# A two-layer graph kernel: another order for the last four tiles of step 0, and a tail with more of its small work on VectorE

## The chip, the cores and the metric

The kernel runs on one core of one Trainium2 chip. The metric is device time in microseconds (us), lower is better: the median of 3 runs before the change is 1654.93 us (1652.97 to 1655.37). Five engines work from queues of their own, each in order: PE (TensorE, matrix products), DVE (VectorE), ACT (ScalarE), POOL (GpSimd, which also issues the gathers and scatters by index) and SP (which issues plain transfers).

## The reference

There are 3327 rows of 256 numbers. Layer 0 is graph attention over a sparse adjacency with a gated update and a layer norm. Layer 1 does two steps of the following, and ends in a layer norm:

```python
def _top_p_attention(X, W1, W2, W3):
    q = X @ W1.T @ W2.T
    k = X @ W3.T
    probs = softmax(q @ k.T)                       # (3327, 3327)
    sp, idx = probs sorted downwards, and its order
    cs = jnp.cumsum(sp, axis=-1)
    keep_sorted = cs - sp < 0.9                    # the nucleus of each row
    A = probs * (mask of what is kept)
    return A / jnp.maximum(A.sum(-1, keepdims=True), 1e-12)

R = (adj + I) / row sums;  Z = 0;  Xf = Xa = X
for n in range(2):
    A = _top_p_attention(Xa, W1, W2, W3)
    Xf = R @ Xf
    Xa = A @ Xa
    Z = Z + Xf @ U1[n].T + Xa @ U2[n].T
out = layernorm(X + Z)
```

## The kernel before, in words

The rows are cut into 26 tiles of 128 (the last has 127). The code orders every engine's queue by the order in which instructions are recorded (`manual_schedule`), so the order of the text, made by generators that yield to each other, is the order on each engine.

**Step 0** (`sparse`, `parts_0`, `step_0`). The attention of this step is so peaked that a tile of rows needs at most 640 columns. A tile goes through some 50 named parts: logits (`logits`, `copy`, on PE and ACT), the nucleus limit (`settle_1`, `settle_2` on DVE), which columns anybody needs (`sign`, `count`, `places`, `hot_l/h/b` on DVE, `placed` on PE, `node` on ACT), the list written to memory and read back in another layout (`told` on DVE, then two SP transfers; `index` on POOL), five gathers (`needed0..4`, POOL, L1598), then `turned` (PE transposes L1623), `turned_copy` (ACT L1630), `by_nodes` (PE L1637), `weights` (ACT L1645), `kept` (DVE L1650), `attention` (PE L1656), `one_over` (DVE), `xa` (ACT L1669), `qk0..3` (PE and ACT: q and k of step 1 for these rows), and `xa_u`, `c_out`, `c_add` (the product with U2: PE L1421, ACT L1690, POOL L1695). `ORDER_0` gives each part a tick; `sparse` starts a tile every 32 ticks (`EVERY0`), so part p of tile t comes at tick 32t + its own. `order_0(t)` makes exceptions for the last four tiles (NT is 26): `SOONER` puts their gathers at other ticks, `LATER` moves `c_add`, and for the last two tiles `KEPT_BACK` parts are left for after step 0. Beside the last tiles, `first_1` records the logits of step 1's first two tiles (`some_logits`: PE L1759, ACT L1762) and the eight largest of each group (`largest`: DVE L1775), each chunk of columns when enough tiles are done (`self.done`).

**Step 1** (`run`, the loop over `i`). Each of 26 tiles (i = 26 to 51) is one `product`: seven groups of transposes (`turn`, L2045, ACT copy L2047) and matmuls (`times`, L2061) with `xu`; between the groups, in seven `slots`, the other work is recorded: logits of tile i+3, the largest of i+2, and for i+1 the short list (`list_1`, `list_2`), the flag of rows that could not be settled by it (`told`, POOL L1820 to L1825), the masking of p (`mask`: DVE match_replace L1957, then a scalar_tensor_tensor with a sum, L1927), `put_aside_1` (POOL L2113 to L2130, with a small matmul `pos` on PE, L2116) and `put_aside_2` (DVE L2147 computes an index, POOL L2148 scatters the flagged rows' data into the table `left_over`). `one_over` (POOL L1936, L1937) is 1 over a row's sum. `tile_end` is the end of older tiles (layer norms by `by_sums` on ACT and POOL, store). `late` is the turn i = 50, in which the mask of the last tile is made; there the scatter stands between the match_replace and the sum.

**The flagged rows** ("hard" rows) are done again in two blocks of 128, h0 and h1, with longer lists: h0's rows are closed after tile 13, h1's after the last tile. `hard_load(k)` reads the table (SP L2158), makes the index (POOL L2161, L2162) and gathers the rows (POOL L2176). `hard_q`, `hard_exp` make their p. A bound on the threshold is sought in six cuts (`CUTS`): the first `COARSE[k]` of them by `coarse_bound` (four ACT passes over p, L2231, and seven or eight small instructions, L2237 to L2246), the rest by `bound` (one DVE pass over p, L1963, and three small ones). `hard(k)` then makes the list of 72, drops what is out (three match_replace passes, L1957) and sums what is kept (L2301); `hard_end(k)` is the product and the end of the rows; `hard_store` scatters them to the output. `COARSE` is (4, 1). `ends` is the last section: h0 is finished, then h1; `whole` makes one number from all flags (DVE L2523 to L2538, two small matmuls), by which a slow path is taken if any row stayed unsettled. The end of h1's rows is `output_rows`: `scaled`, then two layer norms in which ACT does the passes over the row (L2069, L2036), DVE the moments (L2005, L2007) and POOL the rest (L2070 to L2081).

Of the kernel before, what the change touches and what calls it, by code (L numbers as in the profile page):

```python
# [16 lines left out]
P = 128  # L17
# [76 lines left out]
SOONER = {"needed0": 123, "needed1": 124, "needed2": 125, "needed3": 126, "needed4": 127}  # L94
LATER = {"c_add": 196}


def order_0(t):

    order = [(SOONER.get(name, tick), name) if t >= NT - 2 else (tick, name) for tick, name in ORDER_0]  # L100
    if t >= NT - 2:
        order = [o for o in order if o[1] not in KEPT_BACK]
    elif t >= NT - 4:
        order = [(LATER.get(name, tick), name) for tick, name in order]
    return sorted(order, key=lambda o: o[0])
# [12 lines left out]
COARSE = (4, 1)  # L118
# [1120 lines left out]
class Layer1:  # L1239
# [477 lines left out]
    def first_1(self):  # L1717


        while self.phase <= EVERY0 * (NT - 1) + max(AT_0[k] for k in ("sign0", "sign1", "y_out")):  # L1720
            yield
        v = self.item(NT)
        self.item(NT + 1)
        self.fetch(NT)
        for pair in self.chunks():
            while self.done * P < min(NT * P, HALF + pair[0][1] + LC):
                yield
            for i in (NT, NT + 1):
                self.some_logits(i, pair)
                yield  # L1730
            for i in (NT, NT + 1):
                self.largest(i, pair)
                yield
        for b in range(EB):
            self.neighbour(NT, b)
# [63 lines left out]
    def settle(self, lst, before, last, thr2, r, drop, flag, tag, room=None):  # L1799
# [19 lines left out]
        engine = nc.vector if room_given else nc.gpsimd  # L1819
# [81 lines left out]
    def list_2(self, i):  # L1901
# [8 lines left out]
            v.lst, before[:r], v.last, v.thr2, r, DROP, self.flag[:r, n, v.at : v.at + 1], tag  # L1910
# [21 lines left out]
    def one_over(self, i):  # L1932
# [3 lines left out]
        nc.gpsimd.tensor_scalar(v.rA[:r], v.thr2[:r], 0.5e-12 / TOP_P, v.sA[:r], ALU.mult, ALU.max)  # L1936
        nc.gpsimd.tensor_tensor(v.rA[:r], v.rA[:r], self.minus_one[:r], ALU.pow)  # L1937
# [63 lines left out]
    def moments(self, src, r, tag):  # L2001

        nc = self.nc
        st = self.st.tile([P, nc.vector.BN_STATS_DIM], F32, tag="bn", name=f"bn{tag}")
        nc.vector.bn_stats(st[:r], src)  # L2005
        mv = self.st.tile([P, 2], F32, tag="mv" + tag[0], name=f"mv{tag}", bufs=4)
        nc.vector.bn_aggr(mv[:r], st[:r])  # L2007
        nc.gpsimd.tensor_scalar(mv[:r, 1:2], mv[:r, 1:2], 1.0, LN_EPS, ALU.mult, ALU.add)
        nc.gpsimd.tensor_tensor(mv[:r, 1:2], mv[:r, 1:2], self.power[:r], ALU.pow)
        return mv  # L2010

    def sums(self, h, r, tag):
# [7 lines left out]
        yield  # L2020
        sq = self.st.tile([P, 1], F32, tag="sq" + tag[0], name=f"sq{tag}", bufs=2)
# [7 lines left out]

    def shift(self, mv, r, tag):  # L2030
        shift = self.small("shift", f"shift{tag}")
        self.nc.gpsimd.tensor_scalar(shift[:r], mv[:r, 0:1], mv[:r, 1:2], -1.0, ALU.mult, ALU.mult)
        return shift[:r]

    def normalized(self, h, mv, shift, r):
        self.nc.scalar.activation(h, h, AF.Identity, bias=shift, scale=mv[:r, 1:2])  # L2036
# [35 lines left out]
    def output_rows(self, h, terms, r, tag):  # L2072

        nc = self.nc
        m = self.moments(h, r, f"a{tag}")
        shift = self.shift(m, r, f"a{tag}")
        yield
        self.normalized(h, m, shift, r)
        nc.gpsimd.tensor_tensor(h, h, self.g[:r], ALU.mult)
        for term in terms:  # L2080
            nc.gpsimd.tensor_tensor(h, h, term, ALU.add)  # L2081
        yield
        m = self.moments(h, r, f"b{tag}")
        shift = self.shift(m, r, f"b{tag}")
        yield
        self.normalized(h, m, shift, r)

# [20 lines left out]
    def put_aside_1(self, i):  # L2108
        nc, v = self.nc, self.items[i]
        t = v.at  # L2110
        flag = self.flag[:, 1, t : t + 1]
        flag16 = self.small("flag16", f"flag16_{t}", dtype=BF16)
        nc.gpsimd.tensor_copy(flag16, flag)  # L2113
# [6 lines left out]
        nc.gpsimd.tensor_scalar(v.far, flag, -1.0e6, self.base, ALU.mult, ALU.add)  # L2120
        flagged = self.small("flagged", f"flagged{t}")
        self.flagged16 = self.small("flagged16", f"flagged16_{t}", dtype=BF16)
        if self.flagged is not None:
            nc.gpsimd.tensor_tensor(flagged, self.flagged, flag, ALU.add)
        else:
            nc.gpsimd.tensor_copy(flagged, flag)
        nc.gpsimd.tensor_copy(self.flagged16, flagged)
        self.flagged = flagged
        nc.gpsimd.tensor_copy(v.pay[: v.r, 0:1], self.sh.rowid[: v.r, t : t + 1])
        nc.gpsimd.tensor_scalar(v.pay[: v.r, 3:4], v.lim[: v.r], v.t[: v.r], None, ALU.max)  # L2130
# [22 lines left out]
    def hard_load(self, k):  # L2153
# [7 lines left out]
        nc.gpsimd.tensor_copy(v.idx[:, 0:1], v.pay[:, 0:1])  # L2161
        nc.gpsimd.tensor_scalar(v.idx[:, 1:2], v.pay[:, 0:1], float(N - 1), None, ALU.min)  # L2162
# [19 lines left out]
    def hard_q(self, k):  # L2182

        nc, v = self.nc, self.items[f"h{k}"]
        xt = self.transposed((v.x[:, 0, :],), P, f"q{v.tag}")
# [15 lines left out]
        nc.gpsimd.tensor_scalar(v.top, v.pay[:, 3:4], 1.0001, None, ALU.mult)  # L2201
# [14 lines left out]
    def coarse_bound(self, k, cuts, junk):  # L2216


        nc, v = self.nc, self.items[f"h{k}"]
        less = self.small(f"less{k}", f"less{v.tag}")  # L2220
        nc.gpsimd.tensor_scalar(less, v.pay[:, 2:3], 0.5 * (1.0 - 1e-5), None, ALU.mult)
# [385 lines left out]
```

## Time and profile before

| what | us |
|---|---|
| median of 3 runs | 1654.93 |
| the profiled execution, whole | 1656.51 |
| its span, first to last instruction | 1654.7 |
| first matmul of step 0 (L1396) | at 384.9 |
| last ACT copy of `first_1`'s logits (L1762) ends | at 914.7 |
| first transposes of step 1's products (L2045) start | at 936.4 |
| the last tile's product ends | at 1542.5 |
| the sum that ends h0's masking (L2301) ends | at 1561.2 |
| the same for h1 | at 1622.1 |
| h1's product ends | at 1640.3 |
| the last scatter (L2326) is issued | at 1649.5 |

Times "at" are from the start of the span. The mean granted TensorE clock over the span is 0.925. In rows of the timeline the columns are: start, duration, engine, line, operation, what is written and read, shape, and, in brackets, the idle time of the engine before it and what ended that.

### The profile page before, as it was taken

What the parts mean: (1) busy time and instruction counts of PE and PEld (TensorE: products, weight loads), DVE (VectorE), ACT (ScalarE), POOL (GpSimd) and SP (SyncE); (2) the same over time, 40 slices, a digit from 0 to 9 for tenths busy, and PEclk for the clock granted to TensorE, in tenths of its full rate; (3) what the DMA queues carried; (4) which work ended last, traced back from release to release, by engine and by line L of the source; (5) the groups of instructions that cost most, each with busy time, mean ns of one, the idle gap of its engine ahead of it and who ended that gap; (6) DMA issues with size and microseconds to landing.
All of it is one profiled execution on the core that took longest, in us unless ns stands there. A gap on an engine that the chain in (4) does not pass through costs nothing. (4 is left out here: it accounts for less than half of the span.)

```text
span 1654.7 us, 27171 instructions
## 1 busy us (share of the span) xinstructions
PE 1416.5 (86%) x7743; PEld 968.0 (59%) x7743; DVE 1367.8 (83%) x4873; ACT 1097.3 (66%) x2685; POOL 1045.5 (63%) x1523
## 2 busy tenths in 40 slices
PE   4899999986889999999988799999999999985514
PEld 3756666553555555565554477777777667664413
DVE  5799999537788888888862899999999999985992
ACT  4478888655687888788853566766766677764511
POOL 0366666604576677767753468888888878787331
PEclk7599999996799999999997899999999999997767
DMA  8977776313344344444441122222222222211000
GB/s 260 325 246 257 256 258 169 82 53 105 99 124 125 110 121 120 132 111 121 119 125 49 36 60 62 66 72 69 74 71 71 67 59 72 65 53 29 21 4 5
DMA packets 101637, 178.80 MB, mean 108 GB/s; under 512 B 25976, under 2 KB 64119, under 8 KB 101479
## 3 DMA queue, kind: packets, MB, share of 16 engines
q0 software_dynamic: 26288, 73.75, 17.4%
q1 hardware_dynamic: 61818, 93.49, 17.2%
q10 hardware_dynamic: 13372, 9.76, 1.8%
q8 instruction: 63, 1.03, 0.3%
q14 instruction: 96, 0.78, 0.2%
HBM read 139.92 MB, written 37.07 MB: 107 GB/s over the span
## 5 line engine op out<-in xcount | busy, mean ns | idle before, releaser
L2061 PE MATMUL pav<-xu,at 128*128 128x256 f32 (+2 forms) x1352 | 339.2, 396 | 21.9 <-ACT at L2047 21.9
L2061 PEld LDWEIGHTS pav<-xu,at 128*128 128x128 f32 (+2 forms) x1352 | 249.4, 194 | 114.7 <-issue 43.4
L1762 ACT COPY array<-pl 128x416 f32<-128x416 f32 (+3 forms) x402 | 184.1, 512 | 127.8 <-PE pl L1759 127.6
L1775 DVE MAX8 cand<-array 128x8 f32<-128x104 f32 (+5 forms) x1233 | 260.5, 286 | 9.5 <-ACT array L1762 9.1
L1759 PE MATMUL pl<-kT,qT 64*128 64x416 f32 (+3 forms) x804 | 204.4, 567 | 9.4 <-ACT array L1762 8.3
L667 POOL DMA_INDIRECT g<-x_rows,edge x130 | 137.0, 1054 | 46.1 <-issue 32.5
L667 POOL DMA_INDIRECT g<-whx,edge x130 | 135.3, 1041 | 46.9 <-issue 37.3
L2047 ACT COPY at<-pt 128x512 f32<-128x512 f32 (+2 forms) x182 | 95.4, 539 | 103.7 <-PE pt L2045 103.6
L667 POOL DMA_INDIRECT g<-y_rows,edge x130 | 137.1, 1054 | 37.0 <-issue 36.0
L1598 POOL DMA_INDIRECT g<-x1k,uidx x130 | 136.9, 1053 | 33.8 <-issue 25.0
L935 DVE FIND_INDEX8 at<-ones,array 128x8 uint32<-128x840 f32 (+1 forms) x104 | 105.9, 1027 | 0.0
L1759 PEld LDWEIGHTS pl<-kT,qT 64*128 64x128 f32 (+1 forms) x804 | 66.6, 187 | 65.6 <-issue 43.8
L1695 POOL TENSOR_TENSOR x<-x,c 128x256 f32<-128x256 f32 (+1 forms) x26 | 18.5, 714 | 84.6 <-ACT c L1690 84.6
L1656 PE MATMUL pav<-g,w 128*128 128x257 f32 (+1 forms) x260 | 64.1, 395 | 3.5 <-DVE w L1650 3.5
L1052 PE MATMUL acc<-g,m 128*128 128x258 f32 (+1 forms) x260 | 63.2, 391 | 0.0
L1986 PE MATMUL pxf<-g,m 128*128 128x256 f32 (+1 forms) x260 | 62.1, 386 | 0.0
L1052 PEld LDWEIGHTS acc<-g,m 128*128 128x128 f32 (+1 forms) x260 | 50.6, 195 | 18.4 <-issue 6.9
L1884 DVE SCALAR_TENSOR_TENSOR cand<-ec,high 128x256 f32<-128x256 f32 (+1 forms) x104 | 56.9, 547 | 2.8
L2094 POOL TENSOR_TENSOR h<-h 128x256 f32<-128x256 f32 (+1 forms) x26 | 55.3, 2127 | 2.0
L691 PE MATMUL pq<-xtq,wkqk 128*128 128x128 f32 (+1 forms) x208 | 36.0, 298 | 23.2 <-ACT xtq L683 16.1
L1656 PEld LDWEIGHTS pav<-g,w 128*128 128x128 f32 (+1 forms) x260 | 48.9, 196 | 10.7 <-DVE w L1650 4.0
L1079 PE MATMUL prz<-wih,hT 128*128 128x512 f32 (+1 forms) x104 | 52.4, 627 | 3.2 <-ACT hT L1072 1.5
(552 smaller groups left out, 3787.9 us busy)
## 6 DMA issues: line engine op xcount, KB each, us to landing
array<-in_adj_dram SPq DMA_DIRECT2D x25, 1248.0 KB
array<-in_adj_dram SPq DMA_DIRECT2D x25, 415.5 KB
members<-m SPq DMA_DIRECT2D x26, 320.0 KB
m<-members SPq DMA_DIRECT2D x26, 320.0 KB
x_rows<-x ACTq DMA_DIRECT2D x25, 128.0 KB
x1k<-x ACTq DMA_DIRECT2D x25, 128.0 KB
xb_rows<-xb SPq DMA_DIRECT2D x25, 128.0 KB
y_rows<-y SPq DMA_DIRECT2D x25, 128.0 KB
```

Source lines behind the costliest of these rows:

```text
L667: self.nc.gpsimd.indirect_dma_start(out=dst[:, b, :], out_offset=None, in_=table[:, :], in_offset=bass.IndirectOffsetOnAxis(ap=self.edge[: ...
L935: nc.vector.max_index(at[:r, g, :], self.ones8[:r], ad[:r, g, :])
L1052: nc.tensor.matmul(acc[:r, : self.WH], m[:, :r], g[:, k, :], start=(k == 0), stop=(k == EB - 1))
L1598: nc.gpsimd.indirect_dma_start(out=v.g2[:, b, :], out_offset=None, in_=sh.x1k[:, :], in_offset=bass.IndirectOffsetOnAxis(ap=v.idx[:, b : b ...
L1656: nc.tensor.matmul(v.acc[:r, : D + 1], v.w[:, b, :r], v.g2[:, b, : D + 1], start=(b == 0), stop=(b == UB - 1))
L1759: nc.tensor.matmul(pl[:r, :w], q[on], self.sh.kT[on, n, s : s + w], start=True, stop=True)
L1762: nc.scalar.copy(l[:r, h * HALF + s : h * HALF + s + w], pl[:r, :w])
L1775: self.nc.vector.max(cand[:r, g * 8 : g * 8 + 8], src[:r, g * group : min(N, (g + 1) * group)])
L1884: nc.vector.scalar_tensor_tensor(v.cand[:r], ec[:r], high[:r, j : j + 1], ec[:r], ALU.is_ge, ALU.mult, accum_out=above[:r, j : j + 1])
L1986: nc.tensor.matmul(acc[:r, :D], v.m[:, b, :r], v.g[:, b, :], start=(b == 0), stop=False)
L2047: nc.scalar.copy(at[:, :full, :r], pt[:, :full, :r])
L2061: nc.tensor.matmul(v.acc[: v.r, :D], at[:k, j - 4 * g, : v.r], V[:k, j, :], start=(j == 0), stop=(j == NT - 1))
```

## The change

It does five things. (1) A table `ENDING` gives ticks of their own to the parts of the last four tiles of step 0, and `first_1` records the early logits at fixed ticks between them. (2) `COARSE` becomes (3, 3): h0 has three coarse cuts rather than four, h1 three rather than one; h1's small instructions of these, its index and its scalars go from POOL to DVE. (3) For the last tile the flag, `put_aside_1` and, for the last two tiles, `one_over` go from POOL to DVE; in the turn i = 50 the scatter of the last tile's flagged rows is recorded ahead of its mask, and the ends of older tiles, gathers and the h1 load are put into other slots. (4) `hard` sums the kept values in two halves, and `whole` is recorded after the first groups of h1's product. (5) The end of h1's rows becomes `last_rows`, mostly on DVE. In `sums` the square pass gets a buffer of its own. Unused helpers are removed. Line numbers of the old kernel are used throughout the text on the prediction.

```diff
-SOONER = {"needed0": 123, "needed1": 124, "needed2": 125, "needed3": 126, "needed4": 127}
-LATER = {"c_add": 196}
+GATHERS = ("needed0", "needed1", "needed2", "needed3", "needed4")
+ENDING = {
+    NT - 4: {"xa_u": 188, "c_out": 194, "c_add": 200},
+    NT - 3: {"xa_u": 203, "c_out": 209, "c_add": 214},
+    NT - 2: dict(
+        zip(GATHERS, range(123, 128)), turned=139, turned_copy=141, by_nodes=143, weights=143, kept=147, attention=150,
+        one_over=153, xa=155, qk0=157, qk1=159, qk2=159, qk3=161,
+    ),
+    NT - 1: dict(
+        zip(GATHERS, range(107, 112)), y_add=113, hot_l=78, hot_h=78, hot_b=79, placed=80, node=83, told=89, index=105, turned=125, turned_copy=127,
+        by_nodes=130, weights=130, kept=134, attention=138, one_over=141, xa=143, qk0=145, qk1=147, qk2=147, qk3=149,
+    ),
+}
-COARSE = (4, 1)
+COARSE = (3, 3)
...
     def first_1(self):
...
-        for pair in self.chunks():
-            while self.done * P < min(NT * P, HALF + pair[0][1] + LC):
+        both, pairs = (NT, NT + 1), self.chunks()
+        for pair, at in zip(pairs, (112, 120, 131)):
+            while self.phase < last + at:
                 yield
-            for i in (NT, NT + 1):
+            for i in both:
                 self.some_logits(i, pair)
-                yield
...
+        while self.done < NT:
+            yield
+        for i in both:
+            self.some_logits(i, pairs[-1])
+        self.largest(NT, pairs[-1])
+        self.highest(NT)
+        self.largest(NT + 1, pairs[-1])
...
     def one_over(self, i):
-        nc.gpsimd.tensor_scalar(v.rA[:r], v.thr2[:r], 0.5e-12 / TOP_P, v.sA[:r], ALU.mult, ALU.max)
-        nc.gpsimd.tensor_tensor(v.rA[:r], v.rA[:r], self.minus_one[:r], ALU.pow)
+        if i + 2 < STEPS * NT:
...
+        else:
+            nc.vector.scalar_tensor_tensor(v.rA[:r], v.thr2[:r], 0.5e-12 / TOP_P, v.sA[:r], ALU.mult, ALU.max)
+            nc.vector.reciprocal(v.rA[:r], v.rA[:r])
...
     def put_aside_1(self, i):
+        engine = nc.vector if t == NT - 1 else nc.gpsimd
-        nc.gpsimd.tensor_copy(flag16, flag)
+        engine.tensor_copy(flag16, flag)
...
     def hard_load(self, k):
+        engine = nc.vector if k else nc.gpsimd
-        nc.gpsimd.tensor_copy(v.idx[:, 0:1], v.pay[:, 0:1])
+        engine.tensor_copy(v.idx[:, 0:1], v.pay[:, 0:1])
...
     def hard(self, k):
+        halves = self.small("sA2", f"sA2{tag}", 2)
+        for h in range(2):
+            p = v.p[:, h * HALF : min(N, (h + 1) * HALF)]
+            nc.vector.scalar_tensor_tensor(p, p, t, p, ALU.is_ge, ALU.mult, accum_out=halves[:, h : h + 1])
-        nc.vector.scalar_tensor_tensor(v.p, v.p, t, v.p, ALU.is_ge, ALU.mult, accum_out=sA)
+        nc.vector.tensor_tensor(sA, halves[:, 0:1], halves[:, 1:2], ALU.add)
...
+    def last_rows(self, v, x1):
+        h = v.h = self.work.tile([P, 2, D], F32, tag="xt", name=f"h{v.tag}", bufs=3)[:, 0, :]
+        nc.gpsimd.tensor_tensor(x1, x1, self.b, ALU.add)
+        nc.vector.scalar_tensor_tensor(h, v.acc[:, :D], v.rA, v.h1, ALU.mult, ALU.add)
+        for tag in "ab":
+            nc.vector.bn_stats(st, h)
+            nc.vector.bn_aggr(mv, st)
+            nc.gpsimd.tensor_scalar(mv[:, 1:2], mv[:, 1:2], 1.0, LN_EPS, ALU.mult, ALU.add)
+            nc.gpsimd.tensor_tensor(mv[:, 1:2], mv[:, 1:2], self.power, ALU.pow)
+            nc.vector.tensor_scalar(h, h, mv[:, 0:1], mv[:, 1:2], ALU.subtract, ALU.mult)
+            if tag == "a":
+                nc.vector.tensor_tensor(h, h, self.g, ALU.mult)
+                nc.vector.tensor_tensor(h, h, x1, ALU.add)
...
     def ends(self, first, open_ends):
-        for _ in self.coarse_bound(1, CUTS[: COARSE[1]], self.items["h1"].other):
+        coarse = self.coarse
+        for _ in range(COARSE[1]):
+            for _ in range(4):
+                next(coarse)
+            for _ in range(2):
+                next(first, None)
+            next(coarse, None)
             more()
...
-        self.whole()
         while open_ends:
             more()
         self.hard_store(0)
-        for _ in self.hard_end(1):
+        product = self.hard_end(1)
+        next(product)
+        self.whole()
+        for _ in product:
             pass
...
     def run(self):
                     if late:
                         slot(1, next, aside)
-                        slot(2, next, aside, None)
-                        slot(3, self.mask, i + 1, lambda: self.put_aside_2(i + 1))
+                        slot(1, next, aside, None)
+                        slot(2, self.put_aside_2, i + 1)
+                        slot(3, self.mask, i + 1)
...
-                    for b, g in enumerate((0, 0, 0, 3, 3) if late else (0, 0, 0, 4, 5)):
+                    for b, g in enumerate((2, 2) if late else (0, 0, 0, 4, 5)):
                         slot(g, self.neighbour, i + 1, b)
+                else:
+                    for b, g in zip(range(2, EB), (2, 3, 4)):
+                        slot(g, self.neighbour, i, b)
```

## The prediction

> **What bounds the kernel now.** I read the waits first, then the granted clock in short windows, then the timeline of every engine in two stretches (848 to 945 us and 1480 us to the end), and last the chain of waits. Between them, in step 1, the queues keep their order (only the buffer of one ACT pass changes), so those 590 us should move as one block. The first stretch is bound by PE's order. These are PE's rows of the timeline there:
>
> ```profile
> 863.16 0.90 PE L1623 MATMUL pk<-ident,g 128*65 128x128 f32 x3 [3.26 <-DMA g<-x1k,uidx]
> ...
> 889.73 3.37 PE L1656 MATMUL pav<-g,w 128*128 128x257 f32 x10 [1.77 <-DVE w L1650]
> ...
> 902.36 4.65 PE L1656 MATMUL pav<-g,w 128*127 128x257 f32 x10 [1.77 <-DVE w L1650]
> ...
> 910.67 3.47 PE L1759 MATMUL pl<-kT,qT 64*128 64x416 f32 x8
> ```
>
> Tile after tile, transposes, products, exp, mask and attention follow each other with little between them; PE waits for DVE and ACT, and the attention L1656, 2.33 elsewhere (839.40, 854.73), takes 3.37 and 4.65. The windows say why (second number PE's busy time, near the end PE's clock):
>
> ```profile
> 880.00:888.00 8.00, 6.96 (x34) 3.91 (x33) 4.39 (x25) 4.17 (x12) 2.00 (x2) 1.00 0.26 71
> 888.00:896.00 8.00, 4.71 (x15) 3.20 (x16) 1.15 (x3) 2.15 (x6) 5.46 (x6) 0.69 0.23 68
> 896.00:904.00 8.00, 5.78 (x22) 4.80 (x22) 0.82 (x1) 2.29 (x7) 0.56 (x1) 0.50 0.15 33
> 904.00:912.00 8.00, 7.54 (x21) 4.41 (x20) 0.32 (x2) 1.95 (x6) 0.00 (x0) 0.74 0.15 40
> ```
>
> The tail is bound by DVE, which makes h0's and then h1's threshold. What DVE waits for from 1486 on (us, times, longest):
>
> ```profile
> DVE bnah L2005 <- POOL hh L2070: 17.8, 1, 17.8
> DVE cndh L2258 <- POOL 0.7071067811865476_19201 L2246: 11.4, 1, 11.4
> DVE idx L2147 <- POOL far L2120: 8.2, 1, 8.2
> ...
> DVE cndh L2258 <- POOL toph_0.0625_19529 L2246: 1.6, 1, 1.6
> ```
>
> The 17.8 is h1's product on PE. The 8.2 is the last tile's flag, late on POOL; the 11.4 is POOL's coarse cut, behind the scatter. The timeline shows how POOL loses time:
>
> ```profile
> 1500.12 3.68 DVE L1927 SCALAR_TENSOR_TENSOR p<-p,t 127x3327 f32<-127x3327 f32 x1
> ...
> 1500.35 3.50 POOL L2127 CAST flagged<-flagged 128x1 bf16<-128x1 f32 x1
> ...
> 1507.08 2.72 POOL L2148 DMA_INDIRECT left_over<-pay,idx  x1 [0.28 <-issue]
> ...
> 1513.03 0.32 SPq L2158 DMA_DIRECT2D payh<-left_over  x1
> ...
> 1515.62 3.59 POOL L2161 CAST idxh<-payh 128x1 uint32<-128x1 f32 x1 [0.36 <-DMA payh<-left_over]
> ...
> 1519.78 1.12 POOL L2176 DMA_INDIRECT xh<-xa_rows,idxh  x1 [0.28 <-POOL idxh L2162]
> ...
> 1521.21 3.20 POOL L2176 DMA_INDIRECT xh<-x_rows,idxh  x1 [0.31 <-issue]
> ```
>
> A POOL instruction begun during a long DVE scalar_tensor_tensor ends with it (3.50 for a cast that else takes 0.19); during match_replace (1470.59) POOL's rows keep their usual length.
>
> **Part 1, the end of step 0: 13.5 us gained.** I laid PE's new queue on the old durations, from L691 of tile 22 (ends 859.7). `placed` of tile 25 (L1574) comes ahead of tile 23's L1623 and waits for DVE L1567 (862.4): 863.4. L1623 to 864.2, copy L1630 0.75, L1637 1.3: 866.5. L1421 twice 1.9, L1610 0.3, attention of 23 2.3: 872.8. Tile 24's L1623 0.75; L680 waits for one_over and xa (0.35 + 0.5): 874.2; L691 behind its copy: 875.6; L1637 1.3: 876.9. From here the early logits fill the gaps: chunk 1 2.2 (L1759 with ACT between), 879.1; attention 24 2.3, 881.4; chunk 2, 883.5; L680, and L1623 of 25, 884.8; L691 and L1637 2.1, 886.9; chunk 3, 889.1; attention 25, 891.4; L1421 1.9, 893.3; L680, half of the next L1421, L691, 2.0: 895.3. q and k go out in 0.8 (L704, L705), and the last chunk's last ACT copy, 3.0 later, ends at 899.2 instead of 914.7: 15.5 earlier.
>
> Tile 25's gathers must land by 884. Its list is written and read in 5.2 (870.34 to 875.53), so from 863.9 by 869.3; their buffer, one of two, comes free with tile 23's attention at 872.8; five at a pitch of 1.3 issue the last at 878.1, and the slowest landing here (858.12 to 863.12) is 5.0: 883.1. One us is left. POOL's y_add and step 1's five gathers go behind them and are done by 887; c_add of tiles 22 and 23, later too, lies in POOL's old 22.4 us of idling before 918.99.
>
> The clock: rows were slower by 6.5 between 885 and 918 (1.0 and 2.3 in the attentions, 1.2 in L1637 at 898.09, 0.7 in L1421, 1.3 in small ones), after waits of at most 1.8. If it falls as low again, 9 are left of the 15.5; if not at all, 15.5. PE waits less but still in pieces of 1: I take off 2, nearer the full clock, as at 872 to 888. The Trainium skill, "TensorE: Matmul & The Clock Gate", section "What's actually happening", puts the gate on idle windows of about 3.4 us; by that rule no wait of 1.8 should have halved the clock, and the gain would be the full 15.5, but the window of 0.50 above speaks against it.
>
> **Part 2, the tail up to h1's first fine cut: 1.5 gained.** DVE ends tile 25's short list at 1487.5 and `gone` at 1488.1. Ten small instructions follow that stood on POOL (1.9 at the pitch of h0's L1820 to L2295, 0.76 for four), with the index 1490.0, `one_over` 0.4, match_replace 3.7, the sum 3.7: DVE is free at 1498.0, where it was 1503.8. PE's `pos` L2116 waits for the flag until 1489.1, a wait of 0.3 instead of 5.6; behind it stand tile 24's products, which end at 1498.7, not 1506.3. The scatter is queued on POOL behind the add L1991, which waits for ACT L1990 behind a copy of a group that PE turns after `pos`: about 1493.4. Scatter to SP's read takes 5.95, the read 2.6: 1501.9. The index is now on DVE, and h0's bound is queued behind it: DVE waits 4, index and cut 0.6: first pass at S = 1502.5, not 1515.48. Bounds: the scatter at its usual 1.1, 1500.9; held by the sum's pass begun at 1494.2, 1505.
>
> From S: three passes at 4.36, not two, 12.9 and `one_over` 0.4; the old rest of h0 37.7 (1524.01 to 1561.68); h1's scalars 0.5; two sets of eight coarse instructions, dependent, at 0.22, 3.5; the second half's start 0.25: S + 55.2. ACT's third cut starts behind the second set at S + 50.8 and takes 6.8: S + 57.7, so DVE waits 2.5; set three and the first threshold 1.9. h1's first pass comes at S + 59.6 = 1562.1, before 1563.62. Cut one has room: h1's gather, if held by the first pass as at 1521.21, lands at S + 6.5; PE and ACT need 21 from there (1522.88 to 1544.55), the cut 7.3: S + 35, and DVE asks at S + 38.7. The Trainium skill, "SBUF — State Buffer", section "Who interferes with whom", says that DVE and GpSimd share one pair of ports under an exclusive lock; that speaks against placing this gather beside a DVE pass. The 3.7 is already in the numbers, hidden by the slack of 3.7; without the lock the slack is 7.4 and the sum the same.
>
> **Part 3, h1 itself: 14.8 gained.** Two passes fewer, 2 x 4.36 = 8.7. Halves: PE's first groups need only the first half, 1.85 earlier, minus 0.2 for the second start; `whole` no longer stands between L2301 and PE (1622.17 to 1623.67: 1.5), but its two matmuls now stand in PE's queue and wait for each other through DVE (0.58 from L2532 to L2537, and hops: 0.85). Net 2.4 (1.5 to 3.3). The end, 1640.33 to the scatter at 1649.53, is 9.2:
>
> ```profile
> 1640.91 0.72 POOL hh L2070
> ...
> 1643.64 0.61 ACT hh L2036
> ...
> 1645.12 0.73 POOL hh L2081
> ```
>
> Now: DVE from PSUM 0.45 (L1406), twice moments and POOL's two (1.6: 1641.66 to 1643.25), one normalization of 256 each (no such row; between 0.15, a small tensor_scalar, and 0.43, L1102: 0.35, near the latter), g and x1 0.45 each, hops: 5.4 to 5.9, take 5.5. Gain 3.7. x1 + b on POOL is hidden by h1's passes; the store is as before.
>
> **Sum.** 13.5 + 1.5 + 14.8 = 29.8. The profiled span, 1654.7, becomes 1624.9; that execution took 1656.51, so 1.8 lie outside the span; the median of the runs is 1654.93, and 29.8 off it gives 1625.
>
> **Rivals.** (a) Step 0 gives most back: the gathers land 3 late (margin 1) and the clock falls as before; 15.5 - 6.5 - 3 = 6, with the tail's 16.3 about 1633. For it: the margin, the 0.50. Against: denser PE. Chance 0.15. (b) The coarse cuts of h1 become the wait: the gather, the PE chain or `tile_end`'s POOL instructions are held twice more (3.7 each), cut one comes 4 late and cuts two and three follow; with the DVE passes stretched by POOL too, 6 to 8 of the tail are lost: 1632. For it: POOL's 3.5s at 1557.88 and 1585.68. Chance 0.15. (c) Slower: step 1 falls into another beat. Its period is 21.88 from 965 to 1206 (L1986 to L1986) and 24.9 from 1295 to 1345, where PE stands behind POOL adds held by DVE passes. If the new start set POOL so from the first tile on, the 11 quick periods would cost 11 x 3.0 = 33: 1658; it decides once 10 tiles do so. Against: all engines shift together and the queues are unchanged. Chance 0.05. The forecast has 0.65; that the parts simply don't act is excluded by the queues' order.
>
> **Numbers.** Range: best ends (15.5; S 1500.9; no third-cut wait, 2.5; 3.3 at PE) give 1654.9 - 29.8 - 2 - 1.6 - 2.5 - 0.9 = 1618; (a) and (b) in full 1640. Within 0.2% (3.3 us, what a measurement here can tell from none) 0.02, slower 0.05, faster 0.93.
>
> **What would show it.** Right: the last L1762 copy of the early logits near 901; DVE's 8.2 gone and the 11.4 turned into about 4 on the read of `left_over`; three passes in h0, three in h1; about 2.5 for the third cut; some 5.5 from h1's product to its scatter. Wrong: a wait on the gathers at tile 25's L1623, a first cut that DVE waits for, a step-1 period over 21.9 in its first half.

## The result, and the profile after

The changed kernel takes 1628.21 us (median of 5 runs, 1627.84 to 1629.77), the kernel before beside it 1654.93 (5 runs, 1652.77 to 1655.73): ratio 0.9841, 95% interval 0.9828 to 0.9855, 26.7 us less. The profiled execution has a span of 1628.0 (1654.7 before). Lines are now those of the changed kernel: L1759 has become L1779, L1656 L1666, L1623 L1633, L1927 L1948, L1957 L1982, L1963 L1988, L2148 L2140, L2158 L2150, L2161 L2154, L2231 L2225.

PE's rows of the timeline at the end of step 0 (start, duration, engine, line, operation, tiles, shape, and the wait ahead of it):

```profile
872.45 2.43 PE L1666 MATMUL pav<-g,w 128*128 128x257 f32 x10
...
887.00 0.71 PE L1633 MATMUL pk<-ident,g 128*65 128x128 f32 x5
...
892.43 2.43 PE L1666 MATMUL pav<-g,w 128*127 128x257 f32 x10
...
898.29 3.47 PE L1779 MATMUL pl<-kT,qT 64*128 64x416 f32 x8
...
923.77 0.16 PE L2108 MATMUL pos<-flag,lower 128*128 128x1 bf16 x1 [5.01 <-POOL flag L2105]
```

The last three attentions take 2.43 each, where the last two took 3.37 and 4.65. The transposes of tile 25 (887.00) show no wait: its gathers had landed. The early logits' last chunk starts at 898.29 instead of 910.67. Behind it PE still waits 5.0 for POOL's flag (6.2 before), and the first product of step 1 starts at 923.8 instead of 936.4. The windows (PE's busy time second, its clock third from the end):

```profile
864.00:872.00 8.00, 7.54 (x22) 4.41 (x20) 0.82 (x1) 2.67 (x8) 2.68 (x4) 0.64 0.30 63
...
888.00:896.00 8.00, 7.41 (x36) 4.83 (x35) 4.30 (x22) 4.22 (x12) 0.96 (x1) 1.00 0.22 45
896.00:904.00 8.00, 8.00 (x24) 3.30 (x22) 3.92 (x22) 5.41 (x12) 0.63 (x1) 1.00 0.17 49
```

PE is at full clock where it was at 0.69 and 0.50, and busy 7.4 and 8.0 of 8; a slow window lies earlier, at 864, behind a wait of 2.8 for DVE (the product of `placed` at 862.3), and others lie behind the early logits: 0.71, 0.65 and 0.57 in the three windows from 904 to 928. What DVE waits for from 1484 on (us, times, longest):

```profile
DVE hh L2330 <- PE pavh L2068: 8.9, 1, 8.9
DVE idxh L2154 <- DMA payh<-left_over: 7.6, 1, 7.6
DVE number L2578 <- PE total L2576: 4.5, 1, 4.5
DVE bothh_0.5_19584 L2231 <- ACT array L2225: 2.9, 1, 2.9
```

The 17.8 on h1's product is 8.9 and 4.5 now, the 8.2 on the last flag has become 0.9 on `pos`, at 1476.3, the 11.4 on POOL's coarse cut has become 7.6 on the table of flagged rows, and h1's third cut is a new wait of 2.9. Why the table is late is in the timeline of all engines there:

```profile
1476.07 1.14 POOL L2140 DMA_INDIRECT left_over<-pay,idx  x1 [0.30 <-issue]
...
1480.35 3.68 DVE L1948 SCALAR_TENSOR_TENSOR p<-p,t 127x3327 f32<-127x3327 f32 x1
...
1480.57 5.96 POOL L2140 DMA_INDIRECT left_over<-pay,idx  x1 [0.25 <-DVE p L1982]
...
1490.11 0.32 SPq L2150 DMA_DIRECT2D payh<-left_over  x1
...
1491.99 3.68 DVE L1988 SCALAR_TENSOR_TENSOR array<-x,cndh 128x3327 f32<-128x3327 f32 x1
```

The scatter is recorded ahead of the mask, but POOL issues it 0.2 behind the start of the sum pass; it takes 5.96 (2.72 before; the scatter of the tile ahead of it, at 1476.07, takes 1.14), the read follows 9.5 after its start (5.95 before), and h0's first pass can start only at 1491.99. The end of h1's rows on DVE:

```profile
1617.28 0.48 DVE L2330 SCALAR_TENSOR_TENSOR hh<-pavh,rAh,xh 128x256 f32<-128x256 f32 x1 [8.93 <-PE pavh L2068]
...
1622.37 0.41 DVE L2338 TENSOR_SCALAR hh<-hh,mvbh 128x256 f32<-128x256 f32 x1 [0.95 <-POOL mvbh L2337]
```

The scatter is issued at 1623.07, 5.8 after the product's end (9.2 before).

To compare traces whose starts differ I use stretches between five marks in DVE's and POOL's rows: A, the last copy `needed` of step 0; M, the match_replace over p of step 1's 23rd tile; C, that of its last tile; F, h1's first fine pass; E, the last scatter to the output. S is h0's first fine pass, and "C + 10" means 10 us after C.

| kernel | A to M | M to F | F to E | C to S | last scatter into `left_over` takes | S to F |
|---|---|---|---|---|---|---|
| before | 562.4 | 142.8 | 85.9 | 27.3 | 2.72 | 48.1 |
| after | 548.5 | 144.8 | 71.4 | 15.3 | 5.96 | 59.7 |

M comes 14.0 earlier (1420.85 to 1406.86; 0.2 of it because A is earlier), the stretch M to F is 2.0 longer, F to E 14.5 shorter: 26.5.

### The profile page after: what moved, and what is told of

It is laid out like the page before. It is cut to its first block, busy times and chain, and to the rows that moved or that the text cites. A ratio compares the mean times of both kernels' runs of the same rounds, so it can differ in the third digit from the quotient of the medians.

```text
span 1628.0 us, 27192 instructions
## 1 busy us (share of the span) xinstructions
PE 1414.7 (87%) x7743; PEld 967.2 (59%) x7743; DVE 1372.0 (84%) x4921; ACT 1103.1 (68%) x2690; POOL 1036.4 (64%) x1484
## 5 line engine op out<-in xcount | busy, mean ns | idle before, releaser
L1779 PE MATMUL pl<-kT,qT 64*128 64x416 f32 (+3 forms) x804 | 205.7, 570 | 9.2 <-ACT array L1782 8.0
L677 POOL DMA_INDIRECT g<-x_rows,edge x130 | 136.9, 1053 | 45.0 <-issue 30.3
L677 POOL DMA_INDIRECT g<-whx,edge x130 | 134.9, 1038 | 46.9 <-issue 37.2
L1779 PEld LDWEIGHTS pl<-kT,qT 64*128 64x128 f32 (+1 forms) x804 | 66.8, 188 | 65.8 <-issue 44.3
L1705 POOL TENSOR_TENSOR x<-x,c 128x256 f32<-128x256 f32 (+1 forms) x26 | 17.7, 684 | 73.5 <-ACT c L1700 73.5
L1062 PEld LDWEIGHTS acc<-g,m 128*128 128x128 f32 (+1 forms) x260 | 50.5, 195 | 18.4 <-issue 7.4
L1666 PE MATMUL pav<-g,w 128*128 128x257 f32 (+1 forms) x260 | 60.9, 380 | 0.0
L2085 POOL TENSOR_TENSOR h<-h 128x256 f32<-128x256 f32 (+1 forms) x26 | 58.7, 2257 | 2.0
L701 PEld LDWEIGHTS pq<-xtq,wkqk 128*128 128x128 f32 x208 | 29.9, 195 | 39.3 <-ACT xtq L693 38.1
```

Of the source, the lines that this page charges most:

```text
L677: self.nc.gpsimd.indirect_dma_start(out=dst[:, b, :], out_offset=None, in_=table[:, :], in_offset=bass.IndirectOffsetOnAxis(ap=self.edge[: ...
L701: nc.tensor.matmul(pq[:, :r], self.wkqk[:, c, h * DA : h * DA + P], xt[:, c, :r], start=(c == 0), stop=(c == DC - 1))
L1062: nc.tensor.matmul(acc[:r, : self.WH], m[:, :r], g[:, k, :], start=(k == 0), stop=(k == EB - 1))
L1666: nc.tensor.matmul(v.acc[:r, : D + 1], v.w[:, b, :r], v.g2[:, b, : D + 1], start=(b == 0), stop=(b == UB - 1))
L1779: nc.tensor.matmul(pl[:r, :w], q[on], self.sh.kT[on, n, s : s + w], start=True, stop=True)
```

## The experiments

They ran in four groups, each with its own runs of the kernel before: e1 to e4 (1654.11), e5 to e8 (1755.23), e9 and e10 (1654.09), e11 and e12 (1751.87). The second and fourth group ran on another chip, where PE is granted less in steady work (0.88 between 500 and 600 in e5, 1.00 there in the first trace) and A comes at 960 and not 858. Times of different chips are compared by their ratio to the kernel before, and the rest by stretches:

| kernel | ratio to before, 95% | A to M | M to F | F to E | C to S | scatter | S to F |
|---|---|---|---|---|---|---|---|
| e1 | 0.9950 (0.9934 to 0.9967) | 549.9 | 144.2 | 86.5 | 28.0 | 2.72 | 49.0 |
| e2 | 0.9893 (0.9877 to 0.9910) | 561.3 | 139.8 | 72.8 | 11.2 | 2.62 | 59.5 |
| e3 | 0.9844 (0.9827 to 0.9860) | 548.9 | 140.6 | 71.6 | 10.6 | 2.61 | 60.4 |
| e4 | 0.9863 (0.9842 to 0.9884) | 547.2 | 146.5 | 74.6 | 15.6 | 5.96 | 59.7 |
| e5 | 0.9882 (0.9864 to 0.9900) | 550.0 | 144.7 | 71.2 | 15.5 | 5.96 | 59.6 |
| e6 | 0.9892 (0.9873 to 0.9912) | 554.4 | 145.5 | 71.3 | 15.5 | 5.96 | 59.7 |
| e7 | 0.9858 (0.9835 to 0.9880) | 551.4 | 135.5 | 77.0 | 15.5 | 5.95 | 50.3 |
| e8 | 0.9929 (0.9912 to 0.9946) | 549.1 | 145.5 | 71.0 | 10.5 | 2.60 | 65.1 |
| e9 | 0.9824 (0.9798 to 0.9850) | 549.1 | 136.0 | 70.7 | 10.5 | 2.60 | 55.7 |
| e10 | 0.9815 (0.9792 to 0.9837) | 553.1 | 135.3 | 76.7 | 10.5 | 2.60 | 50.5 |
| e11 | 0.9852 (0.9827 to 0.9878) | 554.8 | 134.9 | 73.5 | 12.6 | 2.61 | 52.5 |
| e12 | 0.9889 (0.9861 to 0.9917) | 552.5 | 139.9 | 72.3 | 11.2 | 2.62 | 59.7 |

**e1, step 0 alone.** The kernel before with `ENDING`, the new `order_0` and `first_1` of the diff above, and `highest(NT)` left out of `run`, nothing else.

> Kernel before, with only the new order of step 0's last four tiles and of the early logits. Theory: the first product of step 1 starts at about 923.8 as in the changed kernel (before 936.4), step 1 and the old tail move as one block, and the run gains the whole 12.6 us: about 1642 (1641 to 1644). Rival: part of the 12.6 is lost in step 1 or in the old tail, whose waits are on transfers and on another engine: the start comes at 923.8 all the same, but the end gains under 9, above 1646.

Measured: 1645.66, between the two theories (the gain of 8.5 is under the rival's 9). The first product starts at 922.9, and A to C is 617.1 instead of 629.7: the 12.6 are there up to the last tile. The old tail then takes 163.5 from C to E instead of 161.3 and gives 2.2 back, in pieces of under 1 (C to S 0.7, S to F 0.9, F to E 0.6). The profiled execution is 11.7 shorter, the median of its runs 8.5 shorter, with an interval from 5.5 to 10.9.

**e2, the tail alone.** All of the change but those three places.

> Changed kernel with the old order of step 0 and the old early logits. Theory: the tail alone is worth what is left of the changed kernel's gain, 26.5 - 12.6 = 13.9 us: about 1641 (1640 to 1643), with h1's first fine pass at 1564.2 (0.6 later than before) and 14.5 won behind it. Rival 1: the forecast's 16.3 holds for the tail by itself, and the missing 2 us come from its meeting the new start: 1638.5. Rival 2: the two parts share a gain, and the tail alone brings under 11: above 1644.

Measured: 1637.0, 17.1 less than before (14.9 to 20.3): more than the theory's 13.9, nearest to rival 1, the forecast's 16.3. The stretches tell why: F to E is as in the changed kernel within 1.3, M to F is 5.0 shorter, and 4.0 of that lie between C and S, where the same scatter takes 2.62 here. The two parts do not share a gain (8.5 and 17.1 make 25.6 of the 26.7); one instruction's luck lies between them.

**e3, the scatter ahead of POOL's addition.**

```diff
-                slot(2 if i + 1 < total else 5, next, beside, None)
+                slot(2 + (i + 2 == total) if i + 1 < total else 5, next, beside, None)
```

> Changed kernel in which POOL's addition for tile 24 (and the ACT pass before it) is recorded behind the last scatter instead of ahead of it. The scatter is then issued at about 1477.3, beside match_replace, and not at 1480.6, beside the sum pass. Theory A (the held scatter sets h0's start, and h0's start sets the end): the scatter takes about 1.1 instead of 5.96, payh is there at about 1485, h0's first pass starts at about 1485.5 instead of 1492.0, the chain of gathers and copies to h1's first coarse cut moves along, and the run gains 5 to 6.5: about 1622. Theory B (h1's coarse cuts on ACT have become what sets the end): h0's first pass moves as in A, but cut one and cut three do not, DVE's waits for them grow from 0.3 and 2.9 to some 9 in all, and the run gains under 1: 1627.5 to 1628.5.

Measured: the scatter is issued at C + 2.8, ahead of the sum pass (C + 3.6), and takes 2.61; C to S is 10.6 instead of 15.3, h1's first cut and its first fine pass come along, M to F is 4.2 shorter, and DVE's waits for the cuts stay at 0.3 and 2.9. That is theory A, with 4.2 of its 5 to 6.5: POOL waits 2.1 behind the scatter before, so the last one comes 1.1 earlier and not 3.3, and it takes 2.6 and not the 1.1 of the theory. The runs don't show it: 1628.6 against 1628.2 in the first group of runs, and the profiled execution had lost 2.5 ahead of A. e12 shows one reason why they need not.

**e4, the old end of h1's rows** (`output_rows` and its helpers for `last_rows`).

> Changed kernel with the old end of h1's rows (ACT passes and POOL steps instead of VectorE). Theory: from the end of h1's product to its scatter 9.2 instead of 5.8: 3.4 slower than the changed kernel, about 1631.6 (1631 to 1632.5). Rival: the old end's first ACT and POOL steps were hidden or its waits were a matter of the old place, and less than 2 come back: under 1630.3.

Measured: 9.27 from the product's end to the scatter, not 5.82: the 3.4 of the theory. The runs, 1632.9 (1628.5 to 1635.4), agree within their spread.

**e5, the changed kernel again** (and e12, a third time, whose expectation stands with e11).

> The changed kernel again, for a second trace and for runs on the same chip as the three that follow. It tells how far two executions of one program differ ahead of the changed part (the last copy `needed` of step 0, at 858.3 in the first trace) and whether the scatter, begun 0.2 us after the sum pass in the first trace, is held for 6 us again. Theory (which of the two begins first is a matter of a few tenths): median 1627 to 1630, and the stretch from the last tile's match_replace to h1's first fine pass is 75 where the scatter takes 6 and 71 to 72 where it takes 2.6. Rival (the hold has nothing to do with the sum pass): the scatter takes 6 whenever it is behind POOL's addition, and the stretch is 75 in either case.

Measured: 1734.63 (1731.34 to 1737.12) and 1733.86 (1730.69 to 1737.23). In e5 the scatter starts at C + 3.86 and takes 5.96, as in the first trace. In e12, the same program, the timeline of all engines has it 0.17 earlier:

```profile
1585.93 3.71 DVE L1948 SCALAR_TENSOR_TENSOR p<-p,t 127x3327 f32<-127x3327 f32 x1
...
1585.98 2.62 POOL L2140 DMA_INDIRECT left_over<-pay,idx  x1 [0.25 <-DVE p L1982]
...
1591.53 0.32 SPq L2150 DMA_DIRECT2D payh<-left_over  x1
...
1593.51 3.69 DVE L1988 SCALAR_TENSOR_TENSOR array<-x,cndh 128x3327 f32<-128x3327 f32 x1
```

It starts 0.05 after the sum pass and not 0.22, and isn't held: S is 4.3 earlier, M to F 4.8 shorter than in e5. The rival, that it takes 6 whenever it stands behind the addition, has fallen; a start 0.17 earlier or later decides over 4 us. On this chip the ratio to before is 0.988, not 0.984; no trace of the kernel before was taken there, so where the difference lies stays open.

**e6, the first flag ahead of POOL's addition.** The wait of 5.0 ahead of step 1's first product looked like the next thing to remove.

```diff
                     ahead = self.propagate(NT)
-                    for _ in ahead:
-                        pass
+                    next(ahead)
...
             for _ in self.put_aside_1(NT):
                 pass
+            for _ in ahead:
+                pass
```

> Changed kernel in which POOL's addition for the first tile of step 1 (it waits for an ACT pass and then is held by the sum pass of that tile) is recorded behind that tile's flag. Theory A (PE's 5.0 us wait for the flag ahead of step 1's first product is what is left of the price of POOL at this place, and step 1 moves as a block): PE then waits for the sum pass alone, the first transposes start 3.0 earlier, at 62.5 after the last copy `needed` instead of 65.5, and the run gains 3.0: about 1625.2. Theory B (step 1's first turns are limited by the gathers, the list or the logits that come after): the first product starts 3 earlier and the last tile's match_replace under 1 earlier; 1627.5 to 1628.5.

Measured: 1738.05, nothing gained against e5 beside it (1734.63). The wait is gone and the first product starts 65.2 after A instead of 67.2, but the fourth tile's match_replace comes at A + 122.8 against 122.3: theory B as far as that, the pace of the first turns is set by something later than that product. In tiles 21 and 22 the turns then took 25.4 and 26.5 instead of 24.6 and 23.1, and the last tile's match_replace comes at A + 624.7 against 619.6. Neither theory has that loss.

**e7, COARSE (4, 2).**

```diff
-COARSE = (3, 3)
+COARSE = (4, 2)
...
-                    for g in (0, 2, 5) if i + 3 < total else (0, 1, 2, 5, 6):
+                    for g in ((0, 2, 5) if closing < 7 else (0, 2, 3, 5)) if i + 3 < total else (0, 1, 2, 5, 6):
```

> Changed kernel with COARSE (4, 2): h0's fourth cut is done on ACT in step 1's last two turns, h1 has two coarse cuts and four fine passes. Theory A (h1's third cut is a wait and not a saving: DVE waits 2.9 and spends 1.6 on its small steps): h0 needs one pass fewer (4.4), DVE handles cut one and cut two without the third behind them, h1's first fine pass starts at about 1542 instead of 1551.6 and its four passes end at about 1559.4 instead of 1564.9: 5.5 gained, about 1622.7. Theory B (the third cut pays what a pass costs, as the forecast had it, and the fourth cut of h0 comes late behind the scatter or lengthens step 1): the gain is under 1, or a loss: 1627 or more.

Measured: S to F is 50.3 instead of 59.6, and DVE waits for no cut; of this 9.4 the fourth fine pass takes 5.1 back (four passes 18.4, three 13.3), so 4.2 are left to h1's sum below the threshold, and 3.6 to E. Theory A, at two thirds of its size, since POOL's layer norms now lie beside two of the passes and stretch them by 0.4. Runs: 1731.85 (1728.15 to 1737.33) against 1734.63; they overlap. By these rows h1's third cut is worth next to nothing, one pass (4.4) for a wait of 2.9 and small steps of 1.6, and what e7 gains is h0's pass, done on ACT while it has room; the two were not changed one by one.

**e8, all at once.** e3 and e6 together; `COARSE` (4, 3); for h1 in the last turn:

```diff
-                            slot(3 * g, next, oldest, None)
-                        slot(g + 4, next, held, None)
+                            slot(4 + g, next, held, None)
+                            slot(6 * g, next, oldest, None)
...
-                    for g in range(5):
+                    q = self.hard_q(1)
+                    for g in (2, 3, 3):
+                        slot(g, next, q, None)
+                    slot(3, self.hard_coarse)
+                    for g in range(4):
                         slot(g, next, first, None)
-                    q = self.hard_q(1)
-                    for g in range(2, 5):
-                        slot(g, next, q, None)
-                    slot(4, self.hard_coarse)
                     for j, pair in enumerate(self.chunks()):
-                        slot((4, 5, 6, 6)[j], self.hard_exp, 1, pair)
+                        slot((4, 4, 5, 5)[j], self.hard_exp, 1, pair)
```

> Changed kernel with five edits together: the first flag ahead of POOL's addition, the last scatter ahead of POOL's addition, ACT's older layer norm and the last tile's h1 taken out of the way of h1's exponentials, h1's scalars ahead of h0's list, and COARSE (4, 3) with the sets of small steps placed where ACT should just have ended. Theory: 3 at the start of step 1, 4 at h0's start, and from h0's start to h1's sum below the threshold 64.7 instead of 72.9, 8.2: 15 together, about 1613 (1611 to 1616). Rival: ACT's and POOL's queues are the bound behind h0's start, h1's first cut does not come before h0's start + 31 or its third waits for POOL, and under 9 are gained: above 1619.

Measured: 1742.83, 8 slower than the changed kernel beside it: the rival. ACT's rows and DVE's waits (line numbers of this kernel):

```profile
1619.59 0.47 ACT L2016 ACTIVATE h<-pxf,rinv 127x256 f32<-127x256 f32 x1 [3.05 <-PE pxf L2013]
...
1623.51 0.47 ACT L2077 ACTIVATE h<-pav,rA 127x256 f32<-127x256 f32 x1 [2.97 <-DMA out_dram<-h]
1623.88 1.67 ACT L2226 ACTIVATE array<-qT,minush_0.0625_19370 128x1664 f32<-128x1664 f32 x1
```

```profile
DVE bothh_0.0625_19466 L2232 <- ACT array L2226: 12.7, 1, 12.7
```

The exponentials are done at 1616.5 as meant, but ACT then waits 3.1 for PE's product `pxf` of the last tile. The copy of the last tile's attention product also stands ahead of the first cut on ACT, and its buffer, one of three, comes free only with the store of the oldest tile, whose layer norm had been put behind. Cut one starts at C + 39.7 instead of C + 32, and DVE waits 12.7. That shows why nothing was gained; it doesn't show the loss of 8. From A to E this execution takes 765.6, e5's 765.9, and it is the shortest of its six: where the median loses 8 stays open.

**e9 and e10, the tail in another order, and e3 with e7.** e9 leaves step 1's start alone, and records the first cut and the exponentials ahead of that copy:

```diff
+            engine = nc.vector if j == 3 else engine
...
                         slot(4, next, load)
+                        slot(6, next, load)
+                        slot(6, next, load)
...
+                    for _ in range(4):
+                        slot(6, lambda: next(self.coarse))
+                    for _ in range(2):
+                        slot(6, next, beside, None)
```

> Changed kernel with another tail, step 0 and its hand-over as they are: the last scatter ahead of POOL's addition; COARSE (4, 3), h0's fourth cut on ACT in step 1's last turns and its small steps on VectorE in the wait for payh; h1's gather ahead of POOL's last addition; h1's scalars ahead of h0's list; h1's exponentials and the first cut on ACT ahead of the last tile's h1 and of the copy that waited for a store in e8; the older layer norm among the exponentials; the sets of small steps behind h0's list, its second and its last sum. Distances from the last tile's match_replace (C). Theory: h0's first pass at C + 10 (15.3 in the changed kernel), ACT's first cut from C + 32 to C + 39.5, no wait of DVE over 1 for a cut, h1's sum below the threshold at C + 73 (88.2), so 15 less than the changed kernel: 1613 on a chip where that takes 1628, 39 to 43 less than the kernel before. Rival: another queue has no room for the earlier cuts (ACT's copy behind a store as in e8, POOL's additions held by DVE's passes): DVE waits over 5 for a cut and the gain over the changed kernel is under 9.

> Changed kernel with two edits that were tried one by one: the last scatter ahead of POOL's addition (e3) and COARSE (4, 2) (e7). Theory: both act on the same queue one after the other, so they add: from the last tile's match_replace to the last scatter 146.4 - 3.75 - 3.6 = 139.0, 7.4 less than the changed kernel: 1621 on a chip where that takes 1628, 32 to 36 less than the kernel before. Rival: with the third cut gone, the first and second set the time, and the earlier start of h0 is lost in front of them: the stretch is 142 or more.

Measured: 1624.78 and 1623.70 where before takes 1654.09, so 29.3 and 30.4 less, against 39 to 43 and 32 to 36 in the theories. From C to E e9 takes 136.9 and e10 137.6 (146.4 in the changed kernel): 9.5 gained in e9 (theory 15; DVE waits 2.6 for cut two, which stood behind a layer norm that waited 6.4 for POOL) and 8.8 in e10 (theory 7.4: they add). But half of e9's runs are 1619 to 1621 and half 1629, and e10's lie between 1620.7 and 1630.8. e10's trace is of the long kind: M to C is 74.3 and not 69.8, A to M 4.5 longer, all in tiles 21 to 24. DVE's waits in that stretch of 81 us:

```profile
DVE high L1900 <- ACT ec L1890: 7.1, 2, 3.6
DVE pay L1907 <- ACT array L1878: 4.1, 2, 2.1
DVE pay L1907 <- ACT p L1878: 2.1, 1, 2.1
```

In the changed kernel's trace the first of them is 2.4 and the second 0.4. ACT has a third pass of a cut per turn there, and the exponentials of the next tile come late. But e7, e8 and e9 have the same pace of cuts, and in their traces the turns of tiles 22 and 23 take 23.0 or 23.1 and 25.2, where e10's take 28.1 and 28.6; and e6, without that pace, has 26.5 in tile 22. So the third pass alone doesn't make the long turns, and they come without it too.

**e11, the fourth cut in the last turn.** e9 with the pace of the cuts as in the changed kernel up to the last turn but one, and cut two ahead of the layer norms:

```diff
-                    for g in (0, 2, 5) if i + 3 < total else (0, 1, 2, 5, 6):
-                        slot(g, go_on, g == 2)
+                    for g in (0, 2, 5) if i + 3 < total else (0, 1, 2, 5, 6) if i + 2 < total else (1, 2, 3, 4):
+                        slot(g, go_on, g == 2 and not late)
```

> As e9, with two differences: step 1 keeps the pace of cuts that the changed kernel has, and h0's fourth cut is done on ACT in the last turn alone, between the copies of tile 24's groups; and the second and third cut of h1 are recorded ahead of the layer norms that waited for POOL's addition. Theory A (the runs of e9 and e10 that were some 9 slower lost it in step 1's tiles 21 to 24, where the third ACT pass per turn made the exponentials and so the lists late): from the last copy `needed` to the last tile's match_replace takes 618 to 620, all runs lie within 5 of each other, h1's sum below the threshold comes at C + 76.5 (C + 79.0 in e9), C to the last scatter is about 134.5, and the run is 11 to 13 below the changed kernel beside it. Theory B (step 1 falls into the slow beat by itself): some of the runs are again 8 to 10 above the others, and so are some of the changed kernel's own.

> The changed kernel a third time, beside e11. It gives the ratio on the same chip, and by the spread of its runs and its trace whether step 1's slow beat in tiles 21 to 24 is met without any edit there. By theory A of e11 its runs lie within 4 of each other (1626 to 1630 on a chip like the first), by theory B some are 8 to 10 higher.

Measured: 1728.0, all six runs within 1727.5 to 1729.5, each below each run of the changed kernel beside it (e12), whose median is 5.9 higher. A to C is 624.6, of which 2.7 lie at the end of step 0, ahead of step 1's first match_replace (against e12). C to E is 138.7, not 134.5: the scatter waits 2.1 for the one before it, as in e9, but that one is itself 2.6 later, so S is at C + 12.6 (10.5 in e9), and F to E is 2.8 longer than in e9. h1's sum below the threshold comes at C + 79.1 and not 76.5. So half of the theory's gain. e12's runs spread over 6.5 (1730.7 to 1737.2), between the 4 of theory A and the 8 to 10 of theory B. e11 beats both kernels on its chip; e9 and e10 have the lowest ratios to before, with runs that spread. That the long runs of e9 and e10 come from the third pass is in line with e11's narrow runs, but not shown: e7 to e9 speak against it as said, no long run of e9 was profiled, and the kernel before spreads over 10 us and more in the same groups (1650.2 to 1660.0, 1748.6 to 1762.4).

## Why the prediction was right, and where it was off

1625 was forecast, 1628.2 measured; by parts 13.5 + 1.5 + 14.8 = 29.8 against 14.0 - 2.0 + 14.5 = 26.5 in the trace.

**Part 1** held. The last early copy ends at 902.3 (forecast "near 901"), the gathers were in time, the period of step 1 stayed at 21.9, and the 12.6 at the first product had become 13.6 by its fourth tile, since the second turn takes 22.0 and not 23.0 (22.0 in e1 too, and 22.9 in e2, which has the old step 0). The forecast didn't have that: in its own term, the last early copy, part 1 gained 12.4 of 13.5, and the turn made up for it. The 2 us taken off for the clock were about right, for another reason than given: the window of 0.50 is gone, but one of 0.64 came at 864, where two products took 2.5 and 3.0. Rival (a) didn't come. e1 shows that this part carries through step 1 by itself.

**Part 2** is the step that failed, above all in one term: "Scatter to SP's read takes 5.95". In the time of the kernel before (14.0 later) DVE was free at 1498.0, as forecast. The scatter came at 1494.6 (forecast 1493.4), the read 9.5 later, and from the read to the index it took 1.6 (forecast 2.6). So S was at 1506.0, not 1502.5, and 1.0 beyond the bound of 1505 set for a held scatter. The prediction had it that a POOL instruction begun during such a pass ends with it. That is so for the cast of 0.19 that it shows, but a held instruction still needs its own time behind the pass, all but 0.1 to 0.2 of it: the scatter was held for 3.46, to the pass's end, and took 2.50 more. Nor is 1.1 "its usual" time: 1.1 is that of the tiles before, while the last scatter takes 2.6 to 2.7 in every trace where it isn't held.

From S on the sum was as laid out: S to F 59.65 (59.6). The third cut's wait was 2.9 (2.5), since four ACT passes take 7.2 and not 6.8. Cut one was ready at S + 38.7, just when DVE asked for it (a wait of 0.3). Its slack of 3.7 was used up behind the gather, not by it: PE's first product on the gathered rows starts at S + 6.4 (forecast S + 6.5), but from there to the last exponential it took 24.9 and not 21. ACT stood 5.7 for POOL's layer norm, which two passes held, ahead of its copy of q; PE waited 4.5 of that, and then had 6.3 of the last tile's products between h1's first and second logits.

```profile
1505.19 3.55 POOL L2041 TENSOR_TENSOR mvbt<-minbt,mvbt 128x1 f32<-128x1 f32 x1
...
1508.78 0.60 ACT L2043 ACTIVATE h<-h,mvbt 128x256 f32<-128x256 f32 x1 [5.74 <-POOL mvbt L2041]
```

e12 shows what the forecast described: with the scatter at 2.62 the stretch M to F is 139.9 (139.8 in e2), 2.8 better than before (forecast 1.5).

**Part 3** held: two passes fewer 8.5 (8.7), halves and `whole` 2.6 (2.4; its terms make 2.3), the end 3.4 (3.7; e4 shows the 3.4).

**Rivals.** (b) was near: the cuts had no slack left, and each us that e3 won came through only because the cuts moved along. (c) named step 1's beat; the slower start didn't come, but longer turns in tiles 21 to 24, worth 4 to 9, are met in e6 and e10 (in e10 28.1 and 28.6 where the changed kernel's trace has 23.0 and 22.5).

## What to carry to other kernels

An instruction of POOL that stands beside a long pass of VectorE with two inputs should be placed so that it starts well before the pass or after it; issued as the pass begins, the scatter here cost over 4 us in some executions and nothing in others, and single traces mislead. When the work of one engine is taken off the chain, the next thing in line on each queue decides: here a buffer that comes free with a store, and ACT's exponentials. A wait seen ahead of a block (e6) is worth nothing if what follows the block's first instruction is late anyway.

## What the hardware showed that was not expected

A held POOL instruction doesn't end with VectorE's pass: it ends with the pass plus its own time, less 0.1 to 0.2. The scatter that starts 0.22 into the pass takes 5.96, which is 3.46 to the pass's end and 2.50 more, nearly the 2.6 that it takes unheld. A gather of the changed kernel, which takes 1.0 to 1.1 elsewhere, ends 0.87 behind its pass (the cast of 0.19 in the kernel before, 0.05):

```profile
1496.35 3.69 DVE L1988 SCALAR_TENSOR_TENSOR array<-x,cndh 128x3327 f32<-128x3327 f32 x1
...
1496.85 4.06 POOL L2169 DMA_INDIRECT xh<-x_rows,idxh  x1 [0.30 <-issue]
```

Whether the scatter is held at all hangs on its start. It starts 0.22 into the pass, and was held, in five traces (after, e4 to e7). One that starts 0.05 into it (e2, e12) or 0.9 ahead of it (e3) takes 2.6, and the pass beside it keeps its 3.7. The Trainium skill, "SBUF — State Buffer", section "Who interferes with whom", says of VectorE's two-port modes that whoever issues first gets the shared ports for the whole instruction and the other blocks fully, and of a VectorE instruction with two inputs in SBUF that it contends with a GpSimd instruction that reads SBUF. The held cases show such contention. But in e3 the pass, begun 0.9 after the scatter, was not blocked (3.69), so the rule of the two-port modes doesn't describe this pair: a scatter seems to need the ports only for a part of its time, which no run here shows directly. Why the last scatter takes 2.6 where those of the other tiles take 1.1 stays open too.

The last two scatters into the table start no closer together than 3.2: they are 3.20 to 3.22 apart in e3, e8, e9 and e11 (1584.04 and 1587.25 in e11), where POOL stands idle for 2.1 between them. And PE's clock fell to 0.64 from 864 to 872, with PE busy 7.5 of the 8, behind a wait of only 2.8; in the kernel before it had fallen to 0.50 behind waits of at most 1.8.
